# Three small moves in a two-layer block: where the maxima's transfers are queued, keys ahead of queries, one tick more for the sorted rows

## The chip, the core and the metric

The kernel runs on one core of a Trainium2 chip. The metric is device microseconds (us) of one launch, lower is better. All data are 32-bit floats.

## The reference

Two layers follow each other on `x` of shape (2, 1024, 128). After each of the four parts the input is added and a layer norm is taken.

```python
# 1: retention, 8 heads, keys 64 wide, values 128 wide
q, k = rotary(x Wq), rotary(x Wk); v = x Wv; g = x Wg
o = ((q k^T) / 8 * decay[h, t - s]) v          # no softmax, causal
x = layernorm(x + (groupnorm(o) * silu(g)) Wo)
# 2: attention with a latent of 64, 16 heads of 8, then one of 4 experts
h = rmsnorm(x); lat = layernorm(h Wdkv)
q, k, v = rope(h Wq), rope(lat Wuk), lat Wuv
a = x + softmax(causal(q k^T / sqrt(8))) v Wo
e = argmax(rmsnorm(a) gate_w + gate_b)         # one expert of four for each token
x = layernorm(x + a + relu(rmsnorm(a) W1[e] + b1[e]) W2[e] + b2[e])
# 3: attention, 16 heads of 8, not causal, two scores set to -1e9
q, k, v = x Wq + bq, x Wk + bk, x Wv + bv
x = layernorm(x + softmax(q k^T / sqrt(8)) v Wo)
# 4: a 128 x 128 weight rounded to -1, 0, 1 times its mean size
x = layernorm(x + x ternary(W))
```

## The kernel before, in words

Part 1 is a stage of its own: 16 chunks of 128 tokens, up to about 240 us into the span. Parts 2 to 4 are the rest, and the change lies there.

**The chain of ticks.** Both attentions are one list of steps, written out in `steps`. A step is (attention a, sequence b, half k of 512 tokens, group g of four heads, half h of 256 queries); 32 steps are of the first attention (a = 0), 32 of the second (a = 1). Each step is cut into items, 208 in all, and `chain_tick` handles one item in each place of a pipeline per tick. In tick t it does this:

- `score` (L86, tile `sc`): TensorE multiplies queries by keys for item t, and VectorE takes row maxima of the product (`parts`, L425 with the causal mask, L430 without).
- `shifted` (tile `sct`): the transposed products of item t - 7 (`AHEAD = 7`), and ScalarE's exponentials (`es`, L485).
- `product` (tile `acc`): exponentials times values of item t - 8. ScalarE copies the result out of its bank (L518 or L521), GpSimd sums (L522).

The softmax needs the maximum of a row before its exponential. A query has 32 rows in `qT` for each head, of which 8 are its dimensions; in row 8 (`ONE`) `kT` holds 1 and `qT` is to hold minus the maximum, so that the `sct` product comes out shifted. When a step's last score is done, `shifts` (L437) makes the 8 columns of maxima, and one tick later `turn` (L444) transposes them and `enter` (L446) brings them to their place: ScalarE copies an 8 x 128 tile (`m_rows`, L450), and a DMA of 4 KB writes it into `qT` (L452). There are 64 such DMAs. In the second attention the maxima of a step whose first item is s are entered in tick s + 4 and read from tick s + 7 on.

**Queues.** A queue takes its transfers in the program's order, and a transfer that waits holds those behind it. SP's queue carries nearly all: `m_rows`, the `spread` of new queries and keys (L280, four DMAs of 64 KB for each 512 tokens of `qT` or `kT`), the experts' weights (`load`, L1233 and L1236, two DMAs of 256 KB for each tile of 128 rows, with a register loaded from `expert_of` first), the rows sorted by expert (`e_in`, L1256) and the output.

**Side work.** Everything else of parts 2 to 4 is written as generators. Before each tick `side_work` lets one step of the first job in each of four lanes run, if its time `at` has come; a `yield n` sets the next step n ticks later, and a job that is past its `by` tick is run out. Three of them matter here. `mla_inputs` makes the first attention's queries and keys. `experts` (L1213 on) scatters the rows to an HBM buffer in the order of their expert (GpSimd's indirect DMA, L1245), reads them back (`e_in`, L1256), yields (L1257), and then transposes them on TensorE (`xg_ps`, L1265) four tiles at a time. It runs twice for sequence 0 with 512 rows (`n == NC`, 7 tiles) and once for sequence 1 with 1024 rows (11 tiles). `attn_inputs` (L1363 on) makes the second attention's queries and keys: two products `lpr` on TensorE, each followed by a ScalarE copy with bias into a tile `dense` (L1393) and by `spread`. It runs for each half of each sequence. For sequence 0 its last step is in tick 80, the tick in which the second attention starts; the two first items there read the keys of half 0, tick 82 the keys of half 1, and the queries of half 1 are read from tick 112 on.

**Banks.** All TensorE results of the ticks go through a ring of 8 banks in the order in which they are asked for; a tick takes nine of them (four `sc`, four `sct`, one `acc`) and more for side work.

Of the kernel before, what the change touches and what calls it, by code (L numbers as in the profile page):

```python
# [18 lines left out]
NC = BT // P  # L19
QT = 2  # L20
BQ = QT * P
RH, RD, RV = 8, 64, 128
NG, GH, HD = 4, 4, 8
HW = 32
ONE, NEG0, NEG1 = 8, 9, 10
# [39 lines left out]
def block_kernel(  # L65
# [13 lines left out]
    nc = tc.nc  # L79
# [5 lines left out]
    def mm(o, lhsT, rhs, start=True, stop=True):  # L85
        nc.tensor.matmul(o, lhsT, rhs, start=start, stop=stop)  # L86
# [13 lines left out]
    for e in range(NE):  # L100
# [6 lines left out]
        out=ahead, in_=ahead, pattern=[[1, P]], compare_op=ALU.is_gt, fill=0.0,  # L107
# [24 lines left out]
    def col(name, i=0, rows_=P):  # L132
        at, _ = COLS[name]
        return cols_sb[:rows_, at + i : at + i + 1]
# [25 lines left out]
    mw, mk, lw = {}, {}, {}  # L160

    def row(name):
        at, n = ROWS[name]
        return rowb[:, at : at + n]
# [7 lines left out]
    def v_heads(b):  # L172
        return v_aug[b][:, :, : NH * VW].rearrange("p t (h w) -> p t h w", w=VW)


    qT, kT = ([early.tile([P, NG, T], F32, name=f"{name}_0")] for name in ("qT", "kT"))
# [4 lines left out]
    def slot(name):  # L181
        return banks[0](name)
# [23 lines left out]
    def transposed(src, name):  # L206

        tp = slot(name)
        n = src.shape[1]
        for c in range(n):  # L210
            nc.tensor.transpose(tp[:, c * P : (c + 1) * P], src[:, c, :], ident)  # L211
        return tp[:, : n * P]

    def by_tile(src, w, name):

        py = slot(name)
        n, n_tiles = w.shape[1], src.shape[1] // P
        for c in range(n_tiles):
            mm(py[:, c * n : (c + 1) * n], src[:, c * P : (c + 1) * P], w)
        return py[:, : n_tiles * n]  # L220
# [21 lines left out]
    def scratch(tag, name, shape=(P, NC, P)):  # L242
        return scratch_of[0].tile(list(shape), F32, tag=tag, name=name)
# [33 lines left out]
    def spread(dst, k, dense):  # L277

        for j in range(GH):
            nc.sync.dma_start(out=dst[dims(j), :, block_of(k)], in_=dense[dense_rows(j), :])  # L280
# [75 lines left out]
    def queries(i):  # L356

        a, b, k, g, h = steps[i]
        return k * (BT // BQ) + h
# [5 lines left out]
    for i, (a, b, k, g, h) in enumerate(steps):  # L365
# [4 lines left out]
        else:  # L370
            for c in range(QT):
                n = (q * QT + c + 1) * P
# [3 lines left out]
            if sum(piece[2] for piece in rest_of) <= BT:  # L376
                at, pieces = 0, []
# [68 lines left out]
    def enter(i, tp):  # L446

        a, b, k, g, h = steps[i]
        rows_of = small.tile([GH * QT, P], F32, tag="m_rows", name="m_rows", bufs=2)
        nc.scalar.copy(rows_of, tp[: GH * QT])  # L450
        at = queries(i) * BQ
        nc.sync.dma_start(out=qT[b][ONE::HW, g, at : at + BQ], in_=rows_of)  # L452

    def diagonal_pair(n_item):
        i, pair = t_items[n_item]
# [42 lines left out]
    def product(n_item, entering):  # L498

        i, pair = t_items[n_item]  # L500
        a, b, k, g, h = steps[i]
        acc = slot("acc")
        if entering is not None:
            turn(entering, acc[:, BQ : BQ + P])
        for r, (lo, at_) in enumerate(pair_of(n_item)):
            for j in range(GH):
                at = (g * GH + j) * VW
                mm(
                    acc[hrows(j), lo:BQ], v_aug[b][:, 2 * pair + r, at : at + HW],
                    es[n_item][:, j, at_ : at_ + BQ - lo], start=r == 0, stop=r == 1,  # L510
                )
        if entering is not None:
            enter(entering, acc[:, BQ : BQ + P])
        if pair == 0 and (h == 0 or by_half(a, b, k)):
            sums[a, b, k, g] = pools["work"].tile([P, BT], F32, tag="oT", name="oT")
        sum_ = sums[a, b, k, g][:, h * BQ : (h + 1) * BQ]
        if pair == 0:
            nc.scalar.copy(sum_, acc[:, :BQ])  # L518
        else:
            part = pools["work"].tile([P, BQ], F32, tag="part", name="part", bufs=2)  # L520
            nc.scalar.copy(part, acc[:, :BQ])  # L521
            nc.gpsimd.tensor_tensor(sum_, sum_, part, ALU.add)  # L522
# [45 lines left out]
    def chain_tick(tick):  # L568
# [24 lines left out]
        if 0 <= ai < n_items:  # L593
            product(ai, entering)
        elif entering is not None:
            tp = slot("m_ps")[:, :P]
            turn(entering, tp)
            enter(entering, tp)
# [5 lines left out]
    with ExitStack() as rc:  # L604
# [29 lines left out]
        at, n = R_CONST["cs"]  # L634
# [330 lines left out]
        with tc.manual_schedule():  # L965
# [47 lines left out]
            n = n_chunks - 1  # L1013
# [199 lines left out]
    def experts(oh, endings_of, quick=False):  # L1213
# [6 lines left out]
        n = oh.shape[1]  # L1220
# [6 lines left out]
        def indirect(c):  # L1227
            return bass.IndirectOffsetOnAxis(ap=found["row_of"][:, c : c + 1], axis=0)
# [14 lines left out]
        for c in range(n):  # L1243
            next(finding, None)
            nc.gpsimd.indirect_dma_start(  # L1245
                out=rows_by, out_offset=indirect(c),
                in_=endings_of[c // NC]["xn"][:, c % NC, :], in_offset=None,
# [6 lines left out]
        bias_1 = found["bias_1"]  # L1254
        rows_in = scratch("e_rows", "e_in", (P, NT, P))
        nc.sync.dma_start(out=rows_in[:, :n_tiles], in_=by_e)  # L1256
        yield 2  # L1257
        xgT = scratch("e_cols", "xgT", (P, NT, P))
        for at in range(0, n_tiles, NC):
            if at and n > NC:  # L1260
# [102 lines left out]
    def attn_inputs(b, k):  # L1363

        at, name = ((0, "k_first"), (T - 1, "k_last"))[k]
        t = kT[b][:, :, at]
        nc.gpsimd.tensor_tensor(t, t, col(name).to_broadcast([P, NG]), ALU.add)
        if k == 0:

            for g in range(NG):  # L1370
                nc.sync.dma_start(
                    out=qT[b][ONE::HW, g, :],
                    in_=causal[:GH, :P].unsqueeze(1).to_broadcast([GH, T // P, P]),
                )
        tp = transposed(x2[b][k], "x2_ps")
        x2T = scratch("joT", "x2T", (P, BT))
        nc.scalar.copy(x2T, tp)
        yield 1
        pv = by_tile(x2T, lw["wv"], "lpv")
        for c in range(NC):  # L1380
            nc.vector.tensor_tensor(
                v_heads(b)[:, k * NC + c, :, :HD],
                pv[:, c * P : (c + 1) * P].rearrange("p (h d) -> p h d", d=HD),
                row("bv").rearrange("p (h d) -> p h d", d=HD),
                ALU.add,
            )
        for dst, w, name, tag in (
            (qT[b], lw["wq"], "bq", "sq"), (kT[b], lw["wk"], "bk", "xn")
        ):
            pr = slot("lpr")  # L1390
            mm(pr, w, x2T)
            dense = scratch(tag, "dense", (P, BT))
            nc.scalar.activation(dense, pr, AF.Identity, bias=bias[name])  # L1393
            spread(dst, k, dense)
        yield 1
# [66 lines left out]
    for b in range(B):  # L1462


        after_ = (0, starts(1, 0, 0))
        by = starts(1, b, 0) - 3
        found_ = [{} for _ in range(NB)]
        made = []
        for ks in ([(k,) for k in range(NB)], [tuple(range(NB))])[b]:
            quick = b == 0 and ks[0] > 0  # L1470
            oh = small.tile([P, len(ks) * NC, NE], F32, tag=f"oh{b}{ks[0]}", name="oh", bufs=1)
            for i, k in enumerate(ks):
                heavy.append(Job(
                    max(ends(0, b, k) + 1, after_[b]), by,
                    choice(b, k, oh[:, i * NC : (i + 1) * NC], found_[k], quick),
                ))
            heavy.append(Job(0, by, experts(oh, [found_[k] for k in ks], quick)))
            for k in ks:
                made.append(Job(0, by + 3, endings(b, k, found_[k], quick), heavy[-1:]))
                closing[k].append(made[-1])  # L1480
        for k in range(NB):
            light.append(
                Job(ends(0, b, NB - 1), starts(1, b, 0) + 1, attn_inputs(b, k), made[k : k + 1])
            )
# [166 lines left out]
```

## Time and profile before

| what | value |
|---|---|
| median of 3 runs | 1075.11 us (1066.61 to 1077.7) |
| the profiled execution | 1074.85 us, span 1073.2 us |
| mean granted TensorE clock | 0.972 |
| TensorE (PE) busy | 1012.6 us, 94% of the span |
| VectorE (DVE) busy | 768.7 us, 72% |
| ScalarE (ACT) busy | 685.8 us, 64% |
| GpSimd (POOL) busy | 458.4 us, 43% |
| issue of one `m_rows` DMA on SP (L452) | 521 / 538 / 630 ns (least, median, most), 64 times |
| copy of one `m_rows` on ACT (L450) | 237 to 256 ns |
| issue of a DMA on ACT's queue | `cols_sb` 428 ns, `swap` 593 and 602 ns (three in all) |

The profile is one execution on the chip. "Busy" of PE is modelled at the ends, since matmuls overlap. In a list of waits, the engine and line left of the arrow waited, and what stands right of it came last. In a timeline the columns are start and duration in us, engine, line, operation, tiles written and read, how many, and in brackets the idle time of that engine before and what ended it; SPq and ACTq are the queue parts of those engines, which issue DMAs. The table by stretches gives, after the stretch in us, its length, the busy time of PE, PE's weight loads, DVE, ACT and POOL, with counts, then the granted clock (PEclk, 1 is full), the share of the DMA engines and GB/s.

### The profile page before, as it was taken

The page shows a single profiled execution, that of the slowest core. Times are in us where ns is not written, and L with a number is a line of the kernel's source. Part 1 is how long each engine was busy: PE and PEld are TensorE (multiplying, and loading weights), DVE is VectorE, ACT ScalarE, POOL GpSimd, SP SyncE. Part 2 cuts the span into 40 slices and gives each one's busy share as a digit, 9 for nine tenths or more (in the row PEclk, how much of TensorE's full clock was granted, in tenths as well). Part 3 has the DMA queues.
Part 4 walks back from the last instruction along what each step waited for, and adds up shares of the span by engine and source line. Part 5 has one row for each costly group of instructions (what it writes and reads, how often), then busy time and mean ns, then how long its engine had stood idle before and what let it go on. Part 6 is the DMA issues. An engine that isn't in the chain of part 4 may idle for free.

```text
span 1073.2 us, 28623 instructions
## 1 busy us (share of the span) xinstructions
PE 1012.6 (94%) x11455; PEld 721.6 (67%) x11455; DVE 768.7 (72%) x1747; ACT 685.8 (64%) x1482; POOL 458.4 (43%) x626
## 2 busy tenths in 40 slices
PE   6999999997899999989999999999999999999995
PEld 5888888875565657765776666677756666666662
DVE  4667686667774867777677787766686888888861
ACT  2555544544575767665767677766676777777774
POOL 2466554533354664465444334425271222222222
PEclk9999999998897999999999999999999999999997
DMA  6522122110100032103311000323102000000000
GB/s 207 141 63 50 40 49 48 24 31 2 39 2 17 6 82 87 39 14 84 93 38 23 3 2 7 102 61 100 29 24 41 2 13 2 13 2 3 11 3 10
DMA packets 31061, 43.10 MB, mean 40 GB/s; under 512 B 4496, under 2 KB 18000, under 8 KB 30800
## 3 DMA queue, kind: packets, MB, share of 16 engines
q1 hardware_dynamic: 29664, 38.89, 14.0%
q0 software_dynamic: 1024, 2.10, 0.7%
q8 instruction: 90, 1.47, 0.6%
q10 hardware_dynamic: 240, 0.29, 0.1%
q14 instruction: 43, 0.35, 0.1%
HBM read 23.83 MB, written 4.46 MB: 26 GB/s over the span
## 4 chain that ended last, share of the span: by engine, by line
PE 74%; DVE 11%; POOL 5%; DMA 4%; issue 2%; ACT 2%; SPq 1%; POOLq 0%; DVEq 0%; ACTq 0%
PE sc L86 17%; PE acc L86 16%; PE sct L86 14%; DVE spare L425 3%; PE ph L86 2%; PE pmoe L86 2%; PE pout L841 2%; PE py L86 2%; PE pr L86 2%; PE pv L86 2%; DVE parts L430 2%; PE o_ps L211 1%; PE mpr L86 1%; PE pg L86 1%; PE psc L86 1%
## 5 line engine op out<-in xcount | busy, mean ns | idle before, releaser
L485 ACT ACTIVATE es<-sct 128x512 f32<-128x512 f32 (+1 forms) x832 | 418.4, 587 | 171.5 <-PE sct L86 150.1
L430 DVE TENSOR_REDUCE parts<-sc 128x1 f32<-128x512 f32 x640 | 397.6, 682 | 105.1 <-PE sct L86 90.1
L86 PE MATMUL sc<-kT,qT 32*128 32x512 f32 (+3 forms) x1792 | 423.1, 585 | 8.7 <-DVE parts L425 5.0
L86 PE MATMUL sct<-qT,kT 32*128 32x256 f32 (+1 forms) x3328 | 409.4, 389 | 3.9 <-DMA qT<-m_rows 3.9
L86 PEld LDWEIGHTS sct<-qT,kT 32*128 32x128 f32 x3328 | 292.5, 187 | 23.7 <-issue 7.9
L522 POOL TENSOR_TENSOR oT<-oT,part 128x256 f32<-128x256 f32 x144 | 104.6, 727 | 331.9 <-ACT part L521 331.4
L86 PE MATMUL acc<-es,v_aug 128*32 128x256 f32 (+1 forms) x3328 | 220.4, 382 | 10.5 <-DVE parts L430 4.2
L86 PEld LDWEIGHTS sc<-kT,qT 32*128 32x128 f32 x1792 | 154.6, 189 | 78.8 <-issue 25.9
L86 PEld LDWEIGHTS acc<-es,v_aug 128*32 128x32 f32 x3328 | 89.7, 111 | 105.8 <-DVE parts L430 40.5
L425 DVE CUSTOM_DVE_ANT_0 spare<-sc,causal 128x128 f32<-128x128 f32 (+3 forms) x256 | 125.6, 491 | 45.0 <-PE sct L86 11.6
L909 ACT ACTIVATE og<-pt,cols_sb 128x128 f32<-128x128 f32 x124 | 45.0, 467 | 43.3 <-PE pt L896 43.3
L493 POOL TENSOR_SCALAR_AFFINE_SELECT es<-es 128x512 f32<-128x512 f32 x64 | 40.3, 635 | 62.7 <-ACT es L485 60.9
L521 ACT COPY part<-acc 128x256 f32<-128x256 f32 x144 | 56.9, 395 | 7.7 <-PE acc L86 6.1
L140 POOL TENSOR_TENSOR rstd<-rstd,nhalf 128x4 f32<-128x4 f32 (+2 forms) x46 | 55.5, 1208 | 3.7
L778 POOL TENSOR_TENSOR qd<-qk,r_rest 128x512 f32<-128x512 f32 x16 | 20.3, 1271 | 49.1 <-DVE qk L775 46.2
L795 ACT COPY v<-pv 128x1024 f32<-128x1024 f32 x16 | 16.2, 1012 | 38.6 <-PE pv L86 38.6
L772 POOL TENSOR_TENSOR swap<-swap,r_cs 128x1024 f32<-128x1024 f32 x15 | 35.4, 2360 | 10.7 <-DMA swap<-plain 10.7
L86 PE MATMUL py<-r_wo,og 128*128 128x128 f32 x256 | 33.1, 285 | 2.5 <-DVE og L994 2.5
L86 PEld LDWEIGHTS py<-r_wo,og 128*128 128x128 f32 x256 | 31.3, 200 | 3.7 <-PE pg L86 1.1
L86 PE MATMUL pv<-r_wv,xT 128*128 128x512 f32 x64 | 30.6, 601 | 2.2 <-DVE qk L768 2.0
L841 PE MATMUL pout<-v,sm 128*128 128x128 f32 x256 | 31.5, 277 | 1.2 <-DVE sm L809 1.2
L86 PE MATMUL pg<-xT,r_wg 128*128 128x128 f32 x256 | 31.4, 276 | 1.1 <-ACT v L795 1.1
(236 smaller groups left out, 1262.8 us busy)
## 6 DMA issues: line engine op xcount, KB each, us to landing
e_w<-in_m_w SPq DMA_DIRECT2D x50, 256.0 KB
swap<-plain SPq DMA_DIRECT2D x62, 128.0 KB
qT<-dense SPq DMA_DIRECT2D x32, 64.0 KB
kT<-dense SPq DMA_DIRECT2D x32, 64.0 KB
x<-in_x SPq DMA_DIRECT2D x4, 256.0 KB
mcs<-in_m_const SPq DMA_DIRECT2D x4, 256.0 KB
qT<-m_rows SPq DMA_DIRECT2D x64, 4.0 KB
e_in<-by_expert SPq DMA_DIRECT2D x2, 448.0 KB
```

What stands on the lines that cost most here:

```text
L86: nc.tensor.matmul(o, lhsT, rhs, start=start, stop=stop)
L140: nc.gpsimd.tensor_tensor(r, r, nhalf[:, :n], ALU.pow)
L425: nc.vector.tensor_tensor_reduce(out=spare[:, :n], in0=sc[:, at : at + n], in1=causal[:, BT - n :], scale=1.0, scalar=-3.0e38, op0=ALU.add ...
L430: nc.vector.tensor_reduce(part, sc[:, at : at + n], AX.X, ALU.max)
L485: nc.scalar.activation(es[n_item][:, j, :n], sct[:, :n], AF.Exp, scale=scale)
L493: nc.gpsimd.affine_select(out=d, in_=d, pattern=[[0, GH], [1, P]], compare_op=ALU.is_ge, fill=0.0, base=0, channel_multiplier=-1,)
L521: nc.scalar.copy(part, acc[:, :BQ])
L522: nc.gpsimd.tensor_tensor(sum_, sum_, part, ALU.add)
L772: engine.tensor_tensor(swap[n], swap[n], table(n, 1), ALU.mult)
L778: nc.gpsimd.tensor_tensor(qd[n], rq[n], gq, ALU.mult)
L841: nc.tensor.matmul(pout[n][:, a, g, :], sm[:, a, g, :], v[n][:, 2 * g + a, :], start=opens(n) and g == 0, stop=True, skip_group_check=True,)
L909: nc.scalar.activation(to, of, AF.Identity, bias=bias_, scale=weight)
```

## The change

Three lines are touched. The DMA of the maxima is issued on ScalarE's queue, straight after ScalarE's copy. In `attn_inputs` the keys are made and spread before the queries. In `experts` the wait between the reading of the sorted rows and their transposes is 3 ticks for the 1024 rows of sequence 1, and stays 2 for the 512 rows of sequence 0.

```diff
 def enter(i, tp):
         nc.scalar.copy(rows_of, tp[: GH * QT])
         at = queries(i) * BQ
-        nc.sync.dma_start(out=qT[b][ONE::HW, g, at : at + BQ], in_=rows_of)
+        nc.scalar.dma_start(out=qT[b][ONE::HW, g, at : at + BQ], in_=rows_of)
...
 def experts(oh, endings_of, quick=False):
         nc.sync.dma_start(out=rows_in[:, :n_tiles], in_=by_e)
-        yield 2
+        yield 2 if n == NC else 3
...
 def attn_inputs(b, k):
         for dst, w, name, tag in (
-            (qT[b], lw["wq"], "bq", "sq"), (kT[b], lw["wk"], "bk", "xn")
+            (kT[b], lw["wk"], "bk", "xn"), (qT[b], lw["wq"], "bq", "sq")
         ):
```

In the built order the rest of the 1024-row `experts` job, its `endings` and the two `attn_inputs` of sequence 1 stand one tick later (the last of them in tick 142 instead of 141; the attention that reads them starts in tick 144). [...]

## Prediction

> **What bounds the kernel now.** First the shares of busy time: TensorE 94% of a span of 1073.2 us, the next engine 72%. So only time in which TensorE stands still, or runs slowly, can be won. Second, its waits from 300 to 1040 us, by what ended them. Three kinds end with a transfer:
>
> ```profile
> PE sct L86 <- DMA qT<-m_rows: 3.9, 3, 1.8
> ...
> PE xg_ps L1265 <- DMA e_in<-by_expert: 1.8, 1, 1.8
> ...
> PE sc L86 <- DMA kT<-dense: 1.0, 1, 1.0
> ```
>
> That is five waits, 6.7 us in all: three for maxima, one for sorted rows, one for keys. They are exactly the three transfers that the change touches. The chain of work that ended last passes through all five (start, length); the two not shown are maxima too, 393.48 for 3.49 and 501.29 for 5.30:
>
> ```profile
> 327.38 3.90 DMA qT<-m_rows
> ...
> 585.04 4.98 DMA kT<-dense
> ...
> 691.07 6.32 DMA e_in<-by_expert
> ```
>
> Third, the table by stretches, cut where TensorE's granted clock changes. Its 13th to 15th columns are clock, DMA share and GB/s.
>
> ```profile
> 333.20:346.80 13.60, 13.60 (x75) 7.43 (x73) 3.87 (x6) 6.52 (x14) 5.05 (x4) 0.50 0.01 2
> 398.00:401.50 3.50, 3.50 (x32) 1.34 (x25) 1.29 (x2) 2.17 (x4) 2.63 (x5) 0.51 0.96 267
> 507.30:510.70 3.40, 3.40 (x26) 1.63 (x26) 0.72 (x3) 1.66 (x4) 3.04 (x5) 0.50 0.85 294
> 592.60:596.00 3.40, 3.40 (x26) 1.80 (x26) 1.68 (x3) 1.48 (x4) 0.81 (x2) 0.50 0.00 0
> 698.40:701.80 3.40, 3.40 (x28) 2.34 (x24) 1.48 (x3) 1.63 (x4) 0.00 (x0) 0.50 0.53 159
> ```
>
> These are all the half-speed stretches between 290 and 1055 us. TensorE waited until 331.41, 397.11, 506.73, 590.16 and 697.52; half speed begins at 333.2, 398.0, 507.3, 592.6 and 698.4. Each stretch follows one of the five waits within 2.5 us, and TensorE is busy all through each of them. So a wait costs twice: its own length, and half of the stretch behind it.
>
> **The change part by part.** All sums are against the profiled execution's own time, 1074.85 us; the median of the runs shown, 1075.11, is the same within 0.3 us.
>
> *Maxima on ScalarE's queue, gain.* Why were they late? SP takes its transfers in order:
>
> ```profile
> 324.41 2.87 SPq L280 DMA_DIRECT2D qT<-dense  x4
> 327.38 0.56 SPq L452 DMA_DIRECT2D qT<-m_rows  x1
> ```
>
> ScalarE had copied these maxima by 322.25, but SP waited for new queries from GpSimd, issued their four transfers, and only then this one: 5.1 us lost. At 393.48 the copy had ended at 388.80, at 501.29 at 498.88. Issued 0.03 us after the copy (SP does so where it is free: copy to 949.22, issue 949.25) and landing as late as the slowest of the three, 5.3 us, they are there at 327.6, 394.1 and 504.2. TensorE began to wait at 331.41 - 1.85 = 329.6, at 395.9 and at 505.85. All three waits go. First wait: 1.85 and half of 13.6, 8.65 in all. As a check, the same two ticks of the second `mla_inputs` take 9.53 us (exponentials starting at 377.10 and 386.63), these took 18.17 (325.74 to 343.91), with two groups of four transposes more, about 1.2; that gives 7.4. I take 8.0. Second: 1.17 + 1.7 = 2.9. Third: 0.88 + 1.7 = 2.6. Together 13.5.
>
> *The same edit, cost.* 64 issues leave SP, where 0.54 us each cost nothing (it mostly waits), and come onto ScalarE. The trace shows ScalarE issuing only at the start:
>
> ```profile
> 10.31 1.24 ACTq L758 DMA_DIRECT2D swap<-plain  x2
> 11.59 1.01 ACT L751 COPY plain<-pr 128x1024 f32<-128x1024 f32 x1 [1.31 <-PE pr L86]
> ```
>
> The second copy's input was done at 11.02 and it began when both issues were over: an issue holds ScalarE, for 0.6 us. For 4 KB I take SP's 0.54, since SP's own issues of `swap` (0.51 to 0.82) and of `m_rows` (0.52 to 0.63) hardly differ. Behind it stand the copy of `acc` and the next exponentials. In a plain tick:
>
> ```profile
> 948.97 0.25 ACT L450 COPY m_rows<-acc 8x128 f32<-8x128 f32 x1
> 949.13 0.36 ACT L518 COPY oT<-acc 128x256 f32<-128x256 f32 x1
> 950.17 2.06 ACT L485 ACTIVATE es<-sct 128x512 f32<-128x512 f32 x4 [0.68 <-PE sct L86]
> ```
>
> After the change: issue to 949.79, copy to 950.15, exponentials at 950.17 as before. It just fits; the idle 0.68 us is the cover. The bank of `acc` is next written by the tick's last `sc`, which begins at 950.25, 0.1 us after the late copy. GpSimd, which sums the copy, has idled 331.4 us before such sums in all. In some ten places the cover is thinner (0.46 to 0.54): 0.1 to 0.2 each, 1.4 in all. In the opening (250 to 285 us) ScalarE runs without a pause around two of the five: 0.57 each, 1.1. Sum 2.5; bounds 0 and 64 x 0.57 = 36.5. I stand near the low end because the row above is the common one.
>
> *Keys first.* The eight transfers around tick 80 go out from 582.02, queries first; the keys' four start at 585.04 and the first lands at 590.02. TensorE could have begun at 589.13. The heads came in one after another: the first half of that tick's products took 590.16 to 592.21, against 0.98 us in the tick before. Then half speed. Price: 1.03 + 1.07 + 1.7 = 3.8. Keys first, they are issued 2.9 us earlier and the last lands by 584.2 + 5.0 = 589.2. The queries, late in their place, are read 30 ticks on. In the other three calls nothing waits for keys; in the last pair `dense` of half 1 waited 1.46 us for half 0's transfers to land, and will again, for whichever pair comes second. No gain there.
>
> *One tick more.* Sorted rows landed at 697.4; TensorE stood 1.78 us, then 3.4 us at half speed: 3.5. With one plain tick (2.94) ahead of the transposes the rows are there. The first edit helps too: the six expert weight loads (686.00 to 690.97) stood behind the maxima issued at 684.13, though GpSimd had finished `expert_of` at 667.35. Freed, they land long before, and the rows go out at about 688, once the scatter (last issue 685.81) is down. What the tick shifts ends in tick 142, 2 ahead of its reader; the last keys would then land near 828, and tick 144's exponentials begin at 830.7. Cost 0; if that cover fails, at most the 4.0 of the keys above.
>
> *New half-speed stretches.* Waits of over 1 us also end at 474.35, 483.16, 487.89, 664.08 and 798.28, and none was followed by half speed here, while shorter ones were. So it seems to depend on where a wait falls, and everything now falls elsewhere. I charge one stretch, 1.7 (bounds 0 and 5 x 1.7 = 8.5).
>
> Sum: 13.5 + 3.8 + 3.5 - 2.5 - 1.7 = 16.6, so 1058.2 us; I say 1058.
>
> [...]
>
> **The rivals.**
>
> 1. *Half speed stays.* The stretches belong to something else that falls there (a burst of transfers: the 2nd and 3rd have 96% and 85% of the DMA engines busy; against it, the 1st and 4th have 1% and 0%). Then only 6.7 + 1.07 are won and 2.5 lost: 1074.85 - 5.3 = 1069.6. Chance 0.12.
> 2. *The maxima are late all the same*, because a transfer on the second queue waits behind the same bytes. For the third wait it needs 505.85 - 498.9 = 6.95 us to landing, where 5.3 is the longest seen. Then 3.8 + 3.5 - 4.2: 1071.8. Chance 0.06.
> 3. *A new wait on ScalarE.* [...] Chance 0.08.
> 4. *Slower: the issue is on the path.* If ScalarE's late copies hold TensorE's banks in most ticks, 64 issues cost up to 36.5, so 1074.85 - 20.8 + 36.5 + 1.7 = 1092. It decides from (20.8 - 1.7) / 64 = 0.30 us for each issue on: the cover would have to be that much short in every tick. Chance 0.10.
>
> **How the numbers follow.** The forecast has 0.64. Its own range is 1051 (8.65 for the first wait, the other gains whole, no cost: 1074.85 - 21.4 = 1053.4, and 2 us for scatter, since the runs shown reach 8 us below the profiled one) to 1065 (all five later waits followed by half speed, 8.5 for 1.7). The range given reaches 2 us further down and, up, over rivals 3 and 1: 1049 to 1071. About 1% (1064) is what a measurement of this kernel can tell from no change. Faster: the forecast's 0.64 less a tail of 0.04, rival 3 half, 0.04, and a part of 4 with a small price, 0.03: 0.67. Slower: most of rival 4, 0.07. Same: the rest, 0.26.
>
> **What would show it.** Right: no TensorE wait on `m_rows`, `e_in` or `kT`; clock 1.0 from 290 to 1055 but for one or two stretches; mean clock about 0.985; the exponentials' idle time in ticks with an issue down from 0.68 to near 0.1; weight loads issued near 668. Wrong: TensorE waiting on ScalarE's copies (`part`, `oT`) or an issue of more than 0.9 us on ScalarE; half-speed stretches in new places.

## The result, and the profile after

The changed kernel takes 1080.73 us (median of 7 runs, 1079.96 to 1082.35), the kernel before 1073.22 us beside it (7 runs, 1066.61 to 1077.7): a ratio of 1.0069, interval 1.0044 to 1.0094. It became slower by 7.5 us, where 17 us less were forecast. The profiled execution is one of 1080.48 us with a span of 1078.8 us; its mean granted clock is 0.983 (0.972 before). The profile of the kernel before is of one of its slower executions (1074.85 us, where its runs reach down to 1066.61), so a difference between two profiles is not yet one between the kernels.

**What was to go is gone.** In the list of waits no TensorE wait is ended by `m_rows`, `kT` or `e_in` any more. Of the half-speed stretches between 290 and 1055 us, which were five with 27 us in all, one of 3.4 us is left, in a new place. This is its line in the table by stretches (clock in the 13th column, as before):

```profile
479.40:482.80 3.40, 3.40 (x28) 2.30 (x25) 3.08 (x10) 1.08 (x2) 3.32 (x6) 0.50 0.02 5
```

The experts' weight loads moved up as forecast: in the timeline of SP's queue of the kernel after the six stand at 663.90, where they stood from 686.00 on before.

```profile
663.90 4.12 SPq L1236 DMA_DIRECT2D e_w<-in_m_w  x6
682.90 0.39 SPq L1256 DMA_DIRECT2D e_in<-by_expert  x1
```

**What came in its place.** The chain of work that ended last in the kernel after reads as follows; before, PE had 74% and DMA 4%:

```profile
PE 79%; DVE 10%; POOL 5%; ACT 2%; issue 2%; DMA 2%; ACTq 0%; DVEq 0%; POOLq 0%; SPq 0%
```

So the end now hangs on TensorE more than before, though TensorE has no more to compute. The list of waits of the kernel after says on what it waits (engine and line that waited, what came last, us in total, times, longest):

```profile
ACT oT L518 <- ACT m_rows L450: 22.5, 37, 0.6
...
ACT part L521 <- ACT m_rows L450: 9.7, 16, 0.6
...
PEld sc L86 <- ACT oT L518: 7.8, 25, 1.0
...
PEld sc L86 <- ACT part L521: 7.5, 25, 1.5
```

Of the four only the last stands in the list of before, with 0.9 us. The first two are the issue: ScalarE "waits" 0.6 us, 53 times, between its copy of the maxima and its copy of `acc`. The other two are TensorE's weight loads for `sc` held up by that late copy. The plain tick that the prediction took as its example shows how. It began at 948.84 before and begins at 951.47 after. First ScalarE and the weight loads of the kernel after:

```profile
951.61 0.26 ACT L450 COPY m_rows<-acc 8x128 f32<-8x128 f32 x1
951.90 0.54 ACTq L452 DMA_DIRECT2D qT<-m_rows  x1
952.47 0.37 ACT L518 COPY oT<-acc 128x256 f32<-128x256 f32 x1 [0.61 <-ACT m_rows L450]
...
952.90 0.18 PEld L86 LDWEIGHTS sc<-kT,qT 32*128 32x128 f32 x1 [0.26 <-ACT oT L518]
...
953.00 0.18 PEld L86 LDWEIGHTS sc<-kT,qT 32*128 32x128 f32 x1
```

Then the same place of the kernel before, TensorE alone:

```profile
949.61 0.19 PEld L86 LDWEIGHTS sc<-kT,qT 32*128 32x128 f32 x2
...
949.82 0.59 PE L86 MATMUL sc<-kT,qT 32*128 32x512 f32 x2
949.82 0.19 PEld L86 LDWEIGHTS sc<-kT,qT 32*128 32x128 f32 x2
...
950.25 0.59 PE L86 MATMUL sc<-kT,qT 32*128 32x512 f32 x2
```

Before, the third and fourth head's `sc` run side by side ("x2"), each in two records, at 949.82 and at 950.25, and the first weights load at 949.61, 0.12 us after the copy of `acc` had ended at 949.49. After, the fourth head's weights ("x1") load only when the copy has ended at 952.84, and its two passes trail behind the third's. The tick takes 3.50 us instead of 2.93.

**The account.** The starts of each tick's exponentials give a clock for both traces, and the difference can be split by place. Between ticks 7 and 214 the kernel after falls back by 5.6 us:

| ticks | what stood there before | after less before, us |
|---|---|---|
| 21 to 25 | first wait for maxima, 13.6 us at half speed | -9.1 |
| 35 to 39 | second wait for maxima | -1.8 |
| 61 to 64 | third wait for maxima | -1.2 |
| 81 to 85 | keys | -4.4 |
| 112 to 117 | sorted rows | -5.2 |
| all others | the 64 issues, and other things | +27.3 |

So 21.7 us were won in the five places (20.8 were predicted before costs), and 27.3 us lost in all others. This 27.3 is not the price of the issues alone. 1.7 us of it is the new half-speed stretch. And the same account of the runs below, against the same profile, gives a loss in all others of 1.2 us for the second and third edit together, 4.1 for the tick alone and 10.6 for the keys alone, none of which issues a DMA on ScalarE in these ticks; the first edit alone loses 15.4. In ticks 53, 54, 74, 75 and 132 to 134, for instance, the kernel after loses 7.4 us, and the run with the tick alone 5.0; why is open. What the issues cost is better read from runs that differ in the place of the issues only.

### The profile page after: what moved, and what is told of

Same layout as the page of the kernel before. It is cut to its first block, busy times and chain, and to the rows that moved or that the text cites. A ratio compares the mean times of both kernels' runs of the same rounds, so it can differ in the third digit from the quotient of the medians.

```text
span 1078.8 us, 28517 instructions
## 1 busy us (share of the span) xinstructions
PE 1023.1 (95%) x11455; PEld 724.5 (67%) x11455; DVE 768.6 (71%) x1747; ACT 692.8 (64%) x1482; POOL 459.6 (43%) x626
## 3 DMA queue, kind: packets, MB, share of 16 engines
q1 hardware_dynamic: 28896, 38.62, 13.6%
q0 software_dynamic: 1024, 2.10, 0.7%
## 4 chain that ended last, share of the span: by engine, by line
PE 79%; DVE 10%; POOL 5%; ACT 2%; issue 2%; DMA 2%; ACTq 0%; DVEq 0%; POOLq 0%; SPq 0%
PE sc L86 20%; PE acc L86 17%; PE sct L86 15%; DVE spare L425 3%; PE ph L86 2%; PE pmoe L86 2%; PE pout L841 2%; PE py L86 2%; PE pv L86 2%; PE pr L86 2%; PE o_ps L211 2%; PE pg L86 1%; PE psc L86 1%; PE acc L444 1%; PE mpr L86 1%
## 5 line engine op out<-in xcount | busy, mean ns | idle before, releaser
L485 ACT ACTIVATE es<-sct 128x512 f32<-128x512 f32 (+1 forms) x832 | 422.7, 585 | 142.8 <-PE sct L86 126.7
L86 PE MATMUL sc<-kT,qT 32*128 32x512 f32 (+3 forms) x1792 | 442.2, 579 | 11.4 <-DVE parts L425 5.0
L86 PE MATMUL sct<-qT,kT 32*128 32x256 f32 (+1 forms) x3328 | 418.3, 387 | 0.0
L86 PEld LDWEIGHTS sct<-qT,kT 32*128 32x128 f32 x3328 | 287.1, 185 | 19.5 <-issue 1.8
L86 PE MATMUL acc<-es,v_aug 128*32 128x256 f32 (+1 forms) x3328 | 217.5, 378 | 11.3 <-DVE parts L430 4.9
L86 PEld LDWEIGHTS sc<-kT,qT 32*128 32x128 f32 x1792 | 163.2, 185 | 95.5 <-issue 19.6
L521 ACT COPY part<-acc 128x256 f32<-128x256 f32 x144 | 56.1, 390 | 20.8 <-ACT m_rows L450 9.7
L518 ACT COPY oT<-acc 128x256 f32<-128x256 f32 x64 | 24.3, 379 | 27.7 <-ACT m_rows L450 22.5
```

Of the source, the lines that this page charges most:

```text
L485: nc.scalar.activation(es[n_item][:, j, :n], sct[:, :n], AF.Exp, scale=scale)
```

## The experiments

The theory (T) was now: the issue stands between ScalarE's two copies, the copy of `acc` comes 0.55 us late, and TensorE waits for its bank. Its rivals were that ScalarE's time as such is the price, wherever the issue stands (B), and that the transfers on the second queue are slow or make waits elsewhere (C). Each ratio is to the kernel before, run beside it on the same chip. That kernel's median was 1065.39 us beside the first four runs, 1066.13 beside the next four, and 1073.14 and 1073.53 beside the others, so ratios are compared and not times.

### One part alone: the maxima on ScalarE

```diff
-        nc.sync.dma_start(out=qT[b][ONE::HW, g, at : at + BQ], in_=rows_of)
+        nc.scalar.dma_start(out=qT[b][ONE::HW, g, at : at + BQ], in_=rows_of)
```

> Only the first edit (maxima on ScalarE's queue); queries before keys and the wait of 2 ticks as before the change. Theory T: each issue on ScalarE stands between the copy of the maxima and the copy of acc, and the bank of acc is wanted by the fourth sc product of the same tick, so an issue costs TensorE 0.4 to 0.57 us, 64 of them 25 to 36 us; the three late maxima give back 13.5 us. T expects the changed kernel's time plus 3.8 us for the keys and 0 to 3.5 us for the sorted rows: 1084 to 1088 us, 1.0% to 1.4% over the kernel before. Rival K: the loss comes from the other two edits (the keys or the shifted tick collide with something); K expects 1060 us or less.

Measured: 1.008, interval 1.0044 to 1.0115. The loss belongs to this edit.

### The other two parts

The change without the line above: keys first and the tick more, maxima still on SP.

> Only the second and third edit (keys first, three ticks); the maxima stay on SP. T: 3.8 + 3.5 us are won and nothing is lost, about 1066 us, 0.993 of the kernel before; half speed behind the keys and behind the sorted rows is gone, the three stretches behind late maxima are still there. K: no gain, or a loss of some us.

Measured: 0.9945, interval 0.9909 to 0.9981. These two win 6 us. In its profile the half-speed stretches behind the keys and the sorted rows are gone; two behind late maxima remain (329.7 and 391.1, 3.4 us each).

### The issue behind the copy of acc

All three parts, but ScalarE copies `acc` before it issues the DMA. Nothing is taken from ScalarE: the same 64 issues of the same length on the same queue.

```diff
 def enter(i, tp):
-        nc.scalar.dma_start(out=qT[b][ONE::HW, g, at : at + BQ], in_=rows_of)
+        def send():
+            nc.scalar.dma_start(out=qT[b][ONE::HW, g, at : at + BQ], in_=rows_of)
+
+        return send
...
 def product(n_item, entering):
-            enter(entering, acc[:, BQ : BQ + P])
+            send = enter(entering, acc[:, BQ : BQ + P])
...
             nc.gpsimd.tensor_tensor(sum_, sum_, part, ALU.add)
+        if entering is not None:
+            send()
...
```

> The changed kernel, but ScalarE issues the maxima's DMA behind its copy of acc, not ahead of it: the same 64 issues on the same queue, 0.36 us later each. T: the copy is back where it was, 0.79 us into the tick; the issue then lies in ScalarE's idle 0.68 us ahead of the exponentials; all gains stay, so 1073 - 21 + 2 = 1054 us, 0.982 of the kernel before. Rival B: it is ScalarE's added 36 us of time and its late exponentials that cost, wherever the issue stands: 1080 us as the changed kernel. [...]

Measured: 0.9937, interval 0.9906 to 0.9968, against 1.0069 with the issue ahead. The place of the issues is worth 0.0132, about 14 us (10 to 18 by both intervals), 0.22 us for each of 64. (The two ratios come from two chips. By the profiles the kernel after is behind this one by 17.7 us of span, but they are single executions, and the kernel before differs by 7.8 us between these chips.) The timeline of the same tick in this kernel:

```profile
948.95 0.25 ACT L450 COPY m_rows<-acc 8x128 f32<-8x128 f32 x1
949.11 0.36 ACT L521 COPY oT<-acc 128x256 f32<-128x256 f32 x1
949.23 0.53 ACTq L453 DMA_DIRECT2D qT<-m_rows  x1
949.34 0.59 PE L86 MATMUL sc<-kT,qT 32*128 32x512 f32 x2
...
949.58 0.19 PEld L86 LDWEIGHTS sc<-kT,qT 32*128 32x128 f32 x2
...
950.09 0.60 ACT L488 ACTIVATE es<-sct 128x512 f32<-128x512 f32 x1 [0.62 <-PE sct L86]
```

The copy ends at 949.47, the weights load at 949.58 and the heads run side by side again; the issue ends at 949.76, well ahead of the exponentials at 950.09. From tick 162 to tick 206, where eleven maxima are entered and no half-speed stretch lies in either trace, the kernel after is slower than this one by 5.53 us, 0.50 for each. B and C fall, since ScalarE issues as much here and by the same queue. The gain is still smaller than the expected 0.982; that is taken up below.

### Only the three late ones on ScalarE

Otherwise the changed kernel.

```diff
-        nc.scalar.dma_start(out=qT[b][ONE::HW, g, at : at + BQ], in_=rows_of)
+        queue = nc.scalar if i in (9, 13, 25) else nc.sync
+        queue.dma_start(out=qT[b][ONE::HW, g, at : at + BQ], in_=rows_of)
```

> The changed kernel, but only the maxima of the three late steps (the 10th, 14th and 26th) are issued on ScalarE's queue, the other 61 on SP. T and B: the gains of all three edits, 21 us, for three issues of 0.57 us: about 1054 us, 0.982. C: gains lost at the three places if their transfers are slow on this queue, about 1066 us. Other maxima may become late now that things shift; then a wait of TensorE on m_rows shows where.

Measured: 0.9917, interval 0.9887 to 0.9947. Three issues ahead of the copy do no harm that shows, and the gain of the whole change is there, less than expected.

### The dose: two issues ahead of the copy

Each 4 KB transfer is cut into two of 2 KB by heads; otherwise the changed kernel.

```diff
-        nc.scalar.dma_start(out=qT[b][ONE::HW, g, at : at + BQ], in_=rows_of)
+        n = GH * QT // 2
+        nc.scalar.dma_start(out=qT[b][ONE : 2 * HW : HW, g, at : at + BQ], in_=rows_of[:n])
+        nc.scalar.dma_start(out=qT[b][ONE + 2 * HW :: HW, g, at : at + BQ], in_=rows_of[n:])
```

> The changed kernel, with each transfer of maxima cut into two by heads, both issued on ScalarE ahead of the copy of acc: the suspected cost doubled, nothing else added. If the copy's place behind the issue is the cause, every tick with an issue grows by another 0.54 us beside the 0.56 already there, 48 to 64 of them: 26 to 35 us more than the changed kernel, 1.031 to 1.040 of the kernel before, and a plain tick with an issue takes 4.0 us. [...]

Measured: 1.0317, interval 1.0284 to 1.0351. The second issue costs 1.0317 - 1.0069 = 0.0248, 26 us (22 to 31 by both intervals), more than the 14 us of the first. ScalarE in a plain tick of this kernel:

```profile
977.58 0.25 ACT L450 COPY m_rows<-acc 8x128 f32<-8x128 f32 x1
977.87 0.52 ACTq L453 DMA_DIRECT2D qT<-m_rows  x1
978.43 0.52 ACTq L454 DMA_DIRECT2D qT<-m_rows  x1
978.99 0.37 ACT L520 COPY oT<-acc 128x256 f32<-128x256 f32 x1 [1.15 <-issue]
```

The copy begins 1.15 us late. From tick 162 to 206 this kernel loses 11.43 us against the one with the issue behind the copy: 1.04 for each of eleven, twice the 0.50 of one issue. In these ticks the cost goes with the lateness of the copy, one to one. In ticks 7 to 60, outside the five places, one issue costs less: against the first profile of before the kernel after loses 5.4 us there, 1.7 of it the half-speed stretch, and this kernel 10.7. So there the first issue seems in part covered and the second not; by what is open.

### Two issues behind the copy

The same cut, with both issues in `send`.

> The same two issues, both behind the copy of acc. ScalarE then issues until about 1.1 us after the copy's end, 0.46 us past the start of the next exponentials where one issue left them on time. If only the copy's lateness costs, TensorE goes on with a late exponential (it is read some ticks on, and ScalarE has 0.6 us to catch up in the next tick): 0 to 4 us more than with one issue behind the copy, 0.993 to 0.998 of before. If ScalarE's time as such is the price, each of some 50 ticks loses 0.4 us: 1.010 to 1.015.

Measured: 1.003, interval 1.0012 to 1.0048: between the two expectations. From tick 162 to 206 the second issue, 0.52 us long, costs 2.27 us behind the copy, 0.21 for each of eleven; ahead of the copy it costs 5.90, 0.54 for each. Here is where it goes:

```profile
943.42 0.52 ACTq L454 DMA_DIRECT2D qT<-m_rows  x1
943.98 0.52 ACTq L455 DMA_DIRECT2D qT<-m_rows  x1
944.54 2.06 ACT L490 ACTIVATE es<-sct 128x512 f32<-128x512 f32 x4 [0.88 <-PE sct L86]
```

With one issue the exponentials still find 0.62 us of idle time ahead of them, of which 0.33 us is left behind the issue; with two, the second issue ends at 944.50 and they start 0.04 us later, late. Ahead of the copy and behind it, two issues differ by 1.0317 - 1.003 = 0.0287 on one and the same chip, 31 us, some 15 for each set of 64: this agrees with the 14 us above. So ScalarE's idle 0.68 us was a true cover for the exponentials, which hold out for one issue and not for two. It was no cover for the copy.

### The three late ones, behind the copy

> The two findings together: only the maxima of steps 9, 13 and 25 go out by ScalarE, and behind the copy of acc; the others stay on SP; keys first and the tick more as in the change. The three ticks lose their 0.56 us each against the same with the issue ahead of the copy: 0.990 of before (0.987 to 0.993), no TensorE wait on maxima, keys or sorted rows. If the place of so few issues does not matter, 0.992 as with the three ahead of it.

Measured: 0.9925, interval 0.9897 to 0.9952, the same as with the three ahead (0.9917). For three issues the place can't be told in the time. Between ticks 7 and 214 the profile of the changed kernel is 24.5 us behind this one, with one half-speed stretch of 3.4 us in each: the highest measure of the cost, from single executions on two chips. The two kernels with three issues on ScalarE are the fastest found so far, 8 to 9 us below the kernel before and some 15 below the changed one.

### The kernel before once more

> The kernel before, unchanged, profiled once more. If its half-speed stretches belong to the five waits on transfers, all five show again, whatever their lengths. If their place and number are chance from execution to execution, some of the five waits are not followed by one here, the first is 3.4 us and not 13.6, and the span is 5 to 12 us shorter than in the first profile: then the gains read from that profile were its own and not the kernel's.

Measured: this execution took 1066.1 us, span 1064.4. The table by stretches, cut at the same five waits:

```profile
330.40:333.80 3.40, 3.40 (x29) 1.44 (x27) 1.24 (x2) 2.17 (x4) 0.00 (x0) 0.51 0.01 2
391.90:395.30 3.40, 3.40 (x31) 1.06 (x27) 1.29 (x2) 2.26 (x5) 2.50 (x4) 0.50 0.89 257
501.10:504.50 3.40, 3.40 (x26) 1.58 (x27) 0.98 (x2) 1.92 (x4) 2.92 (x5) 0.50 0.79 274
586.40:589.80 3.40, 3.40 (x28) 1.78 (x26) 1.52 (x3) 1.33 (x4) 0.97 (x2) 0.51 0.00 0
690.40:693.80 3.40, 3.39 (x44) 2.31 (x44) 1.67 (x3) 2.18 (x5) 0.00 (x0) 1.00 0.32 80
```

The five waits are there again. The first stretch is 3.4 us and not 13.6, and the wait for the sorted rows (0.94 us here, 1.78 in the first profile) has none. Against this execution the same account of the kernel after gives -14.7 us in the five places and +28.2 in all others. What all others lose is the same, 27 to 28; the gain is 7 us smaller, because this execution had less to give back.

### Keys first alone, and the tick more alone

> The kernel before with the keys' order alone changed. Predicted from the first profile: the wait of 1.03 us on the keys, 1.07 us of heads coming in one after another and half of a 3.4 us stretch go: 3.8 us, 0.9965 of before. If the stretch is there in some executions only, 2.1 to 3.8 us in the median; if the keys are hidden anyway, nothing.

Measured: 0.9989, interval 0.9961 to 1.0017: no difference that can be told. The wait for the keys is gone from its profile, and ticks 81 to 85 win 4.3 us. But all others lose 10.6, 3.4 of it in a new half-speed stretch of 6.8 us that begins at 780.2.

> The kernel before with the tick more for the sorted rows alone. Predicted from the first profile: 1.78 us of wait and half of a 3.4 us stretch go: 3.5 us, 0.9967 of before. The second profile of the kernel before shows this wait at 0.94 us with no half-speed stretch behind it: by that 0.9 us, 0.999. If what the tick shifts runs into the keys behind it, up to 4 us worse, 1.004.

Measured: 0.9935, interval 0.9912 to 0.9957, in the median the largest gain of the three parts, 7 us. The wait for the sorted rows and what followed it are gone. In the trace, against the second profile of before, it gains 3.2 us from tick 112 to 117, where the rows are read, and loses 2.5 us from tick 117 to 162, where the moved steps lie (the second and third edit together lose 2.7 there). So where the median's gain comes from was not settled.

### The maxima alone, issued behind the copy

The first edit alone, with `send` as above.

> The kernel before with one edit: all 64 transfers of maxima on ScalarE's queue, each issued behind the copy of acc. This prices what early maxima are worth once the issue is off the path. The prediction's 13.5 us would give 0.987. If only the first of the three waits (1.85 us and half of the stretch behind it, 1.7 in most executions) is really won, because at 397 and 506 TensorE waits for GpSimd's masks in its place, it is 3 to 4 us: 0.997.

Measured: 0.9961, interval 0.9938 to 0.9983, 4 us. The first edit's gain, free of its cost, is 4 us in the median, not 13.5. Against the same edit with the issue ahead (1.008) the place is worth 0.0119, 13 us: a second measure of the cost. Two of the three waits for maxima are only exchanged for others. This is TensorE's timeline in that kernel, at the places that were 397.11 and 506.73 in the first profile:

```profile
388.68 0.86 PE L86 MATMUL acc<-es,v_aug 128*32 128x256 f32 x16 [1.74 <-POOL es L496]
...
498.75 0.86 PE L86 MATMUL acc<-es,v_aug 128*32 128x256 f32 x16 [2.20 <-POOL es L496]
```

TensorE now waits 1.74 and 2.20 us for GpSimd's masks of the exponentials, where it had waited 1.17 and 0.88 us for maxima. GpSimd's timeline, here from the kernel after, shows why they are late:

```profile
501.93 1.01 POOL L1245 DMA_INDIRECT by_expert<-xn,row_of  x1 [3.33 <-DMA by_expert<-xn,row_of]
502.96 1.23 POOL L493 TENSOR_SCALAR_AFFINE_SELECT es<-es 128x512 f32<-128x512 f32 x2
```

The masks stand behind the third scatter of sorted rows, which waits 3.33 us for an earlier scatter to land. In the kernel before the same stop was there (3.70 us until 507.07), covered by the wait for maxima.

### A tick more between two scatters

The kernel with three late maxima behind the copy, and one more edit:

```diff
                 in_=endings_of[c // NC]["xn"][:, c % NC, :], in_offset=None,
...
-            yield 1
+            yield 2 if n == NC and c == 1 else 1
```

> Three maxima by ScalarE behind the copy, keys first, the tick more, and in the two smaller sorts one tick more between the second and the third scatter of rows. With the maxima early, TensorE waits at 388 and 498 for GpSimd's masks of the exponentials (1.62 and 2.36 us in the same kernel without the edit), and GpSimd is late because its third scatter waits 2.2 to 3.7 us for the second's completion ahead of those masks. If that is what comes next behind the maxima, both waits fall below 0.5 us and the time falls by 4 to 7 us with the half-speed stretches they can cause: 0.986 to 0.989 of before. If the masks are late for another reason, the waits stay and the time is the same: 0.992.

Measured: 0.9924, interval 0.9899 to 0.9949, the same as without (0.9925). The two waits for masks did go: no idle time of TensorE over 0.4 us is left from 342 to 459 us, nor at the second place. But the job's later steps moved, and other waits grew in their place, such as these two:

```profile
462.01 0.66 PE L86 MATMUL acc<-es,v_aug 128*32 128x256 f32 x4 [2.73 <-POOL es L497]
...
555.97 0.42 PE L86 MATMUL acc<-es,v_aug 128*32 128x256 f32 x4 [2.37 <-DVE parts L425]
```

So the cause of the late masks is confirmed, and the mending is worth nothing as done here.

## Why the prediction was wrong

**The step that failed** is *The same edit, cost*: "It just fits; the idle 0.68 us is the cover. The bank of `acc` is next written by the tick's last `sc`, which begins at 950.25, 0.1 us after the late copy." It was priced at 2.5 us with an upper bound of 36.5; by the ratios, the issues cost 14 us more ahead of the copy than behind it (13 with the first edit alone, 25 at most by a pair of profiles), and 0.50 us each in the plain ticks. The writer of the bank was named rightly, its time was not. The row at 950.25 is the second of two records of that product; the first is at 949.82, and its weights load at 949.61. The copy, which the prediction put at 950.15, had to be done by then and had 0.12 us to spare. Reading the tick's records head by head would have shown it: the four `sc` have eight matmul records, in rows of two. The price of an issue was right (0.54 us), the cover that was named, 0.68 us, covers the exponentials, and the two-behind run shows that it does. It stood for the wrong reader. A cover has to be measured to the first one that needs the result.

**The gains failed by about as much.** With the issue behind the copy the whole change wins 7 us (0.9937), where the sum had 20.8 less 1.7 for half speed. So of the 24 us between the forecast (16.6 less) and the result (7.5 more), by the ratios about half are the cost and half the gains. With the gains as forecast, a cost of 14 us would still have left the change 5 us faster. Why the gains were smaller stands below, term by term.

**Rival 4 held** in its mechanism: TensorE waits for banks that ScalarE's late copies hold (its weight loads for `sc` wait 7.8 and 7.5 us for them in the profile after). Its price of 1092 took 0.57 us for all 64; by the ratios each costs 0.22 (0.16 to 0.29), below the 0.30 from which it was to decide alone; the pair of profiles gives 0.38. With the gains that were left, 7 us, either decides. It was given 0.10 because the tick was thought to show a cover, and the cover had been read from one row.

**The maxima's gain, 13.5 us.** The first place, 8.0 predicted, gave 9.1 against the first profile and 4.3 against the second. The other two, 5.5 predicted, gave 3.0 (1.8 + 1.2), since the masks came next. What was late next was not asked there: GpSimd's wait for the scatter, 3.70 us, ended 0.34 us after TensorE's wait for the third maxima, and was in the trace of before to be read.

**Keys, 3.8 us:** 4.4 in the traces, 1.2 in the time of that edit alone (4.2 to -1.8 by its interval). **The tick, 3.5 us:** 5.2 and 2.7 in the traces, 7 in the time. What the tick shifts was charged at nothing; where it lands, from tick 117 to 162, the tick alone loses 2.5 us against the second profile, and the second and third edit together 2.7.

**New half speed, 1.7 us:** one stretch of 3.4 us came, as charged.

**The base of the sum.** The profiled execution was taken for a typical one, since its 1074.85 us are the median's. But the kernel before ran from 1059.29 to 1074.96 us on one chip, and the two profiles differ by 8.8 us in span, of which 13.7 us less at half speed explains 6.8. What an edit can win back by removing a half-speed stretch is the average over executions, not the longest one seen. The long stretch does come again: the kernel with the tick more alone has 13.65 us at half speed from 330.81 on. But the kernels without the cost end between 0.992 and 0.994, 7 to 9 us of gain, where the sum had 20.8 before costs. Rivals 1 and 2 fall: the stretches went with their waits, and no maxima came late. Rival 3, a new wait on ScalarE, falls too: half of its 0.08 is in the 0.67 for faster, and the range reaches up over it, but no run shows such a wait. Of the 64 issues only the first, at 249.47, held ScalarE for long (1.11 us, the next longest 0.58), and the weight loads moved up.

**Short waits, and the second queue.** With the waits of 0.88 to 1.85 us gone, their half-speed stretches are gone. The maxima landed in time by ScalarE's queue, so SP's order was what had held them (5.1 us from 322.25 on), and a second queue did win something: 4 us, in the run with the issue behind the copy. But the issue time was paid on ScalarE instead: 0.54 us, 64 times, ahead of a copy that TensorE waits for, which cost 14 us and the sign.

## What to carry to other kernels

The DMA issues moved onto ScalarE stood in its order for 0.54 us each: put such an issue behind whatever another engine waits for, and measure the slack to the first record of that reader, not to its last. Where a wait is removed, look at what else was due in that time; two of three waits here were only handed on. And take a second profile of the kernel before, if times of its runs spread by a per cent: gains read from one execution's half-speed stretches are that execution's.

## What the runs showed of the hardware

**Half-speed stretches started on a grid of 3.413 us.** In all fourteen profiles, every stretch starts at a whole multiple of 3.413 us from the others in the same profile (off by 0.004 us at most) and lasts 3.413 us or a multiple of it (the last one is cut off by the end). Where the grid lies against the kernel differed from execution to execution: counted from the span's start in steps of 3.413 us, it lies 2.1 us off in the first profile of before and 2.7 us off in the second. For the first: 333.20, 398.05 and 507.28 are 19 and 32 steps apart. Cutting the time from 290 to 1030 us into those steps, TensorE's idle time in a step (no matmul and no weight load) mostly told whether the next ran at half speed, counting steps that are at full speed themselves:

| idle time in the step | steps | followed by half speed |
|---|---|---|
| 1.55 us or more | 14 | 14 |
| 1.25 to 1.55 us | 31 | 5 |
| 0.8 to 1.25 us | 60 | 7 |
| under 0.8 us | 2891 | 2 |

That fits the first profile, where waits of like length were followed by half speed at some places and not at others: the wait of 2.09 us that ends at 474.35 was cut by the grid into 0.88 and 1.21 us, and no half speed followed; of the wait of 1.85 us that ends at 331.41, 1.60 us fell into one step, and half speed followed. Between 0.8 and 1.55 us the idle time alone did not decide, and what did is open.

**The spread differs from kernel to kernel.** The seven runs of the kernel after spread over 2.4 us (1079.96 to 1082.35) and the four with two issues ahead over 2 us (1097.96 to 1099.94); the kernel before spread over 6 to 16 us, by the chip. The kernel with two issues ahead has no half-speed stretch between 290 and 1055 us, the kernel after has one, the kernel before four or five. But the first edit alone, with one such stretch, spread over 6.0 us in ten runs, so what sets the spread is open.
